# Two-layer graph attention: broadcast rows through DRAM in place of TensorE, with signs and roots moved in the order of the queues

## The chip, the core and the metric

The kernel runs on one core of one Trainium2 chip. The metric is the device time of one execution in microseconds. Three runs of the kernel before gave 2392.19, 2395.01 and 2395.21 us, median 2395.01 us. The span in a profile is the time from its first to its last instruction; times in views of the trace count from the span's start.

## What is computed

There are 16 graphs of 1024 nodes with 256 features, one adjacency matrix for all. Each graph goes through a layer normalization and a first network (a matmul to 512 features, a dense attention over all nodes, a matmul back to 256, an attention masked by the adjacency), is added to its input, and then goes through a second normalization and a second masked attention. Cut to what matters:

```python
def _gat(inp, adj_mask, W, a):
    h = jnp.matmul(inp, W)
    f1 = jnp.matmul(h, a[:F_, 0])
    f2 = jnp.matmul(h, a[F_:, 0])
    e = leaky_relu(f1[:, :, None] + f2[:, None, :], ALPHA)
    if adj_mask is not None:
        e = jnp.where(adj_mask[None] > 0, e, NEG_INF)
    return jnp.einsum('bij,bjf->bif', softmax(e, axis=2), h)   # then elu

# network 0 of a graph
out = relu(x @ mlp1_w + mlp1_b)
out = elu(elu(_gat(out, None, W_fc, a_fc))) + out
out = relu(out @ mlp2_w + mlp2_b)
out = relu(elu(elu(_gat(out, adj, W_hand, a_hand))) + out)
# whole: x = x + net0(relu(layernorm(x))); x = x + net1(relu(layernorm(x)))
```

Here net1 is one masked attention with its own W and a, and relu at the end. All is in float32.

## The kernel before, in words

**Tiles.** A graph's 1024 nodes are eight tiles of 128 partitions (`NT = 8`), in two halves of four (`NH = 2`, `TH = 4`). Each graph passes through these objects: `Norm` (two of them), `Dense` (first matmul, dense attention, second matmul), `Gnn0` (masked attention a) and `Gnn1` (masked attention b).

**The masked attentions** need, for every node i, the factor q of i as a row that is the same on all 128 partitions: `weight` (L356, DVE) makes a tile of weights from that row, two columns and the mask `edge`, and `product` (L367, PE) multiplies it by the rows of h. The row is made by `row` (L343): `row_broadcast` (L236) transposes each of eight columns of 128 values, spread over 128 columns, on PE into PSUM, and ACT copies the result to SBUF (L347). Ahead of it stand `extremes` (the largest and smallest f2 on each partition, L318 and L319) and `vectors`: two transposes spread these over all partitions, two reductions on DVE (L328, L329) take the extremes of all, three small exponentials on ACT make the columns `qwd`. The smallest f2 is used only in `trouble`, a flag that is looked at after the last graph.

**The dense attention** of graphs 1 to 15 (and half of graph 0) has no product over all pairs. Nodes are ranked by f2: `columns` (L456) takes f2 as a column, `row` (L460) spreads it as the row `r2` by the same eight transposes and an ACT copy (L466), and finds the largest; `rank` (L484 to L491, DVE, three passes over r2 for each of eight tiles) counts the smaller ones; `scatter` (L498, POOL, indirect DMA) writes the rows of h in sorted order to DRAM; `read_sorted` (L544, SP) reads them back. DVE makes running sums from both ends (L575, L592); SP writes them to DRAM as a table (`write_table`, L584), with carries between partitions (`carry`, L600 to L604). `sign` (L522, ACT, eight times a graph) counts for every node how many f2 lie above minus its f1, from the same r2; `count` (L528) turns this into an index; `gather` (L615, POOL, indirect DMA) fetches from the fine table and then adds from the coarse one; `share` and `mean` (L627 to L639) make the result, and `merge` (L686) transposes it.

**The order of work** is written by hand. `at(lo, hi, steps)` puts steps on a table with nominal times, in us; the table is sorted and the steps are issued in that order, and the instructions of PE, DVE, ACT and SP stay in it. POOL's are chained by hand in the same order (only scatters may pass each other). So every engine and SP's queue take their instructions strictly in the order of the nominal times, and each waits only for its inputs and for free buffers. `PERIOD` is 142: in the period of graph b, PE works on the masked attention a of graph b, the masked attention b of graph b - 1, and parts of the dense attentions of graphs b + 1 and b + 2. The first period is shorter by 28. The lines that place what the change touches:

```python
def dense_begin(t0, b):
    d = dense[b]
    at(t0 - 38.5, t0 - 38.5, [d.columns])
    at(t0 - 31.5, t0 - 31.5, [d.row])
    at(t0 - 28, t0 - 12, each(d.rank, range(NT)))
```

`dense_begin` serves graphs 2 to 15; graphs 0 and 1 have their own lines at the start. In `second_norm` the last two graphs have their own lines too, so `vectors` and `row` of b are split over two periods for graphs 0 to 13. `masked_first` places the two roots of the second norm (`Norm.root`, L257 and L258, POOL) at 36 and 46.5 of graph 0's period; in that period the coarse gathers of the second half stood from 34 on. DVE's `center` (L262) needs the root, and PE's `turn` (L272) needs `center`.

**Buffers.** The rows r2, the rows of a and the rows of b share one tag, `rows`, with two buffers in turn: a row takes the buffer of the row two before it. Matmul results have four PSUM buffers (`mm`), transposes two (`tr`), broadcasts one (`bc`). Weights have eight (`att`).

Of the kernel before, what the change touches and what calls it, by code (L numbers as in the profile page):

```python
# [17 lines left out]
P = 128  # L18
# [13 lines left out]
def fast_path(ctx: ExitStack, tc: tile.TileContext, alarm, x, adj, w1, b1, w2, b2, w_fc, a_fc,  # L32
# [148 lines left out]
    coarse_d = [dram.tile([P + 1, 2 * K], F32, name=f"coarse{k}") for k in range(2)]  # L181
    zero = work.tile([1, K], F32, tag="carry", name="zero", bufs=2)
    nc.vector.memset(zero, 0.0)
    for k in range(2):
        for s in range(2):
            nc.sync.dma_start(fine_d[k][N:N + 1, s * K:(s + 1) * K], zero)
            nc.sync.dma_start(coarse_d[k][s * P:s * P + 1, s * K:(s + 1) * K], zero)

# [44 lines left out]
    def row_broadcast(dst, col):  # L233

        for u in range(len(col)):
            nc.tensor.transpose(dst[:, u * P:(u + 1) * P], col[u].to_broadcast([P, P]), ident)  # L236

# [54 lines left out]
    class Masked:  # L292
# [3 lines left out]
        def __init__(self, get_hT, w_sb, slope, b, which):  # L296
            self.get_hT, self.w_sb, self.slope, self.name = get_hT, w_sb, slope, f"{which}_{b}"
            self.hm = None
            self.att = {}
            self.out = {}  # L300
# [20 lines left out]
        def vectors(self):  # L321
# [4 lines left out]
            row_broadcast(ext_ps[:, :2 * P], cols(self.ext))  # L326
            top = small.tile([P, 4], F32, tag="top", name=f"top{self.name}")
            nc.vector.tensor_reduce(top[:, 0:1], ext_ps[:, :P], AX.X, OP.max)  # L328
            nc.vector.tensor_reduce(top[:, 1:2], ext_ps[:, P:2 * P], AX.X, OP.min)  # L329
# [4 lines left out]
            nc.vector.scalar_tensor_tensor(trouble[:, 1:2], top[:, 0:1], top[:, 1:2],  # L334
# [8 lines left out]
        def row(self):  # L343
            rows_ps = bc_psum(f"rowsps{self.name}")
            row_broadcast(rows_ps, cols(self.qwd[:, 0, :]))
            self.rows = work.tile([P, N], F32, tag="rows", name=f"rows{self.name}")
            nc.scalar.copy(self.rows, rows_ps)  # L347
# [67 lines left out]
    class Dense:  # L415
# [44 lines left out]
        def row(self):  # L460

            b, ext = self.b, self.ext
            r2_ps = bc_psum(f"r2ps_{b}")
            row_broadcast(r2_ps, cols(self.fs[:, 1, :]))
            self.r2 = work.tile([P, N], F32, tag="rows", name=f"r2_{b}")
            nc.scalar.copy(self.r2, r2_ps)  # L466
# [9 lines left out]
            self.place = small.tile([P, NT], I32, tag="place", name=f"place_{b}")  # L476

# [32 lines left out]
        def query(self):  # L510

            f1 = self.fs[:, 0, :]
            self.q = small.tile([P, NT], F32, tag="qd", name=f"qd_{self.b}")
            nc.vector.tensor_scalar(self.q, f1, self.top[:, 0:1], 0.0, op0=OP.add, op1=OP.max)
            nc.scalar.activation(self.q, self.q, AF.Exp, scale=SLOPE_A - 1.0)
            self.signs = small.tile([P, NT], F32, tag="signs", name=f"signs_{self.b}")
# [259 lines left out]
    def dense_begin(t0, b):  # L776
        d = dense[b]
        at(t0 - 38.5, t0 - 38.5, [d.columns])
        at(t0 - 31.5, t0 - 31.5, [d.row])
# [11 lines left out]
    def dense_sums(t0, b):  # L791
        d = dense[b]
        at(t0 - 3, t0 - 3, [d.sums_begin])
        at(t0 + 8.5, t0 + 28, each(d.sign, range(NT)))
# [64 lines left out]
    def second_norm(t0, b):  # L859
# [62 lines left out]
    at(START + 54.2, START + 54.2, [d.row])  # L922
# [28 lines left out]
    at(START + 98.5, START + 98.5, [e.row])  # L951
# [23 lines left out]
    for b in range(NB):  # L975
# [491 lines left out]
```

## Time and profile before

| what | value |
|---|---|
| median of three runs | 2395.01 us |
| the profiled execution's own time | 2395.08 us |
| its span | 2393.4 us, granted TensorE clock 0.987 |
| r2: PE transposes L236, then ACT copy L466 | 128 of 272 ns busy; 16 of 1012 ns |
| rows of b: PE transposes, then ACT copy L347 | 128 of 273 ns busy; 16 of 995 ns |
| extremes: PE transposes for a and for b | 32 of 275 ns and 32 of 276 ns busy |
| reductions of the smallest, L329 | 16 of 281 ns for a, 16 of 281 ns for b |
| sign L522 | 124 of 1146 ns |
| rank passes L484, L486, L488 | 740, 806 and 352 ns |
| gathers L615, fine and coarse | 124 of 1093 ns and 124 of 1577 ns on POOL |
| PE waits in all, centering before a transpose (L272 for L262) | 27.6 us, 20 times, longest 10.4 us |
| SP's DMA queue, packets and share of 16 engines' span | 97440, 24.5% |

A line of a group gives the line of the code, engine, operation, output and inputs, count, busy time and the mean of one, then the idle time of the engine just before these instructions and what ended it. Matmuls overlap, so the busy time of one (272 ns) is more than the distance from one start to the next. A line of a timeline gives start and length in us, engine, line, operation, and in brackets the idle time before it with its releaser. PEld is the load of weights of PE, which runs beside its matmuls. A stretch's line gives its length, the busy time of each engine with counts, then PE's clock, the DMA engines' busy share and GB/s.

### The profile page before, as it was taken

Reading aid. Unit: us, or ns where it says so; the run is one execution under the profiler, and the core shown is the slowest. Engines: PE = TensorE matmul, PEld = TensorE weight load, DVE = VectorE, ACT = ScalarE, POOL = GpSimd, SP = SyncE. Lnnn points to the kernel's source line nnn. Section 1 sums busy time; section 2 is a strip of 40 time slices with the busy share of each in tenths; the row PEclk is TensorE's granted clock in tenths of the full one; section 3 lists DMA queues with packets and bytes.
Section 4 is the critical chain, followed back from the end, with each engine's and each line's share of the span. In section 5 each row is a group of like instructions: output and inputs, shape, how many; then the busy total and the mean of one; then the engine's idle time right before and its main releaser. Section 6 shows DMA issues by size and latency. Waiting matters only on the chain. (4 is left out here: it accounts for less than half of the span.)

```text
span 2393.4 us, 31270 instructions
## 1 busy us (share of the span) xinstructions
PE 2311.4 (97%) x10281; PEld 1788.2 (75%) x10281; DVE 1635.3 (68%) x4531; ACT 1286.1 (54%) x2740; POOL 977.9 (41%) x1216
## 2 busy tenths in 40 slices
PE   8988899999999999999999999999999999999897
PEld 5666687787777878777777868777787877878676
DVE  6665586676858667685866858577685867759554
ACT  4355565545656554565645556564555655455442
POOL 1153335363443536344353533535443453634220
PEclk9999999999999999999999999999999999999898
DMA  4548257372654827356382645737264573726500
GB/s 170 166 141 212 44 153 191 108 190 78 170 143 138 206 89 189 89 153 169 124 220 89 168 97 151 185 122 196 78 182 110 156 189 108 191 74 193 115 1 28
DMA packets 143562, 333.62 MB, mean 139 GB/s; under 512 B 9624, under 2 KB 60824, under 8 KB 139296
## 3 DMA queue, kind: packets, MB, share of 16 engines
q0 software_dynamic: 45952, 163.99, 25.6%
q1 hardware_dynamic: 97440, 167.56, 24.5%
q8 instruction: 84, 1.38, 0.3%
q14 instruction: 86, 0.70, 0.1%
HBM read 205.38 MB, written 126.12 MB: 139 GB/s over the span
## 5 line engine op out<-in xcount | busy, mean ns | idle before, releaser
L367 PE MATMUL oa<-hma,atta 128*128 128x258 f32 x2048 | 459.7, 383 | 7.0 <-DVE atta L356 4.4
L448 PE MATMUL h<-wfc_sb,resT 128*128 128x257 f32 x2048 | 464.6, 380 | 0.0
L367 PE MATMUL ob<-hmb,attb 128*128 128x257 f32 x2048 | 458.3, 383 | 5.4 <-DVE attb L356 5.4
L367 PEld LDWEIGHTS oa<-hma,atta 128*128 128x128 f32 x2048 | 385.6, 191 | 71.9 <-DVE atta L356 10.5
L367 PEld LDWEIGHTS ob<-hmb,attb 128*128 128x128 f32 x2048 | 391.2, 192 | 61.6 <-ACT hmb L351 3.7
L448 PEld LDWEIGHTS h<-wfc_sb,resT 128*128 128x128 f32 x2048 | 379.8, 190 | 52.3 <-issue 1.0
L697 POOL TENSOR_TENSOR resT<-resT,e 128x512 f32<-128x512 f32 x128 | 163.1, 1274 | 415.9 <-DVE e L696 371.9
L356 DVE SCALAR_TENSOR_TENSOR atta<-rowsa,qwda,edge 128x256 f32<-128x256 f32 x512 | 251.2, 519 | 45.2 <-ACT rowsa L347 30.8
L356 DVE SCALAR_TENSOR_TENSOR attb<-rowsb,qwdb,edge 128x256 f32<-128x256 f32 x512 | 257.3, 531 | 30.9 <-PE ob L367 21.4
L391 POOL TENSOR_TENSOR posa<-posa,onat 128x256 f32<-128x256 f32 x120 | 101.0, 841 | 390.2 <-ACT posa L383 390.2
L434 PE MATMUL m<-hT,w_sb 128*128 128x512 f32 x512 | 238.8, 602 | 0.5 <-ACT posa L383 0.5
L704 PE MATMUL m<-resT,w_sb 128*128 128x512 f32 x512 | 230.5, 597 | 4.4 <-POOL resT L697 4.4
L615 POOL DMA_INDIRECT got<-coarse,k x124 | 195.6, 1577 | 42.5 <-issue 36.2
L405 ACT ACTIVATE rb<-ob,recb 128x256 f32<-128x256 f32 x128 | 57.4, 474 | 268.5 <-DVE recb L403 249.0
L688 DVE TENSOR_SCALAR e<-hpT 128x512 f32<-128x512 f32 x128 | 88.4, 691 | 145.7 <-PE hpT L686 144.5
L704 PEld LDWEIGHTS m<-resT,w_sb 128*128 128x128 f32 x512 | 94.1, 192 | 105.8 <-issue 94.3
L450 ACT COPY hnat<-h 128x257 f32<-128x257 f32 x256 | 92.1, 365 | 143.4 <-PE h L448 128.4
L382 ACT ACTIVATE ea<-oa,reca 128x256 f32<-128x256 f32 x128 | 60.6, 473 | 192.9 <-DVE reca L379 192.9
L615 POOL DMA_INDIRECT got<-fine,k x124 | 135.6, 1093 | 68.4 <-DVE reca L379 33.1
L434 PEld LDWEIGHTS m<-hT,w_sb 128*128 128x128 f32 x512 | 93.1, 194 | 84.6 <-issue 82.3
L498 POOL DMA_INDIRECT sorted<-hnat,place x128 | 131.8, 1030 | 39.3 <-issue 16.3
L392 POOL TENSOR_TENSOR ea<-ea,posa 128x256 f32<-128x256 f32 x120 | 112.1, 934 | 85.0 <-ACT ea L389 67.4
(179 smaller groups left out, 3615.6 us busy)
## 6 DMA issues: line engine op xcount, KB each, us to landing
xs<-sorted SPq DMA_DIRECT2D x32, 1028.0 KB
fine<-tt SPq DMA_DIRECT2D x15, 2052.0 KB
fine<-xs SPq DMA_DIRECT2D x15, 2052.0 KB
x<-in_x_dram SPq DMA_DIRECT2D x16, 1024.0 KB
out_dram<-x SPq DMA_DIRECT2D x32, 512.0 KB
xn<-in_x_dram SPq DMA_DIRECT2D x15, 1024.0 KB
coarse<-carry SPq DMA_DIRECT2D x32, 256.5 KB
fine<-tt SPq DMA_DIRECT2D x2, 1026.0 KB
```

The source lines that it names most:

```text
L356: nc.vector.scalar_tensor_tensor(a_t, self.rows[:, q * PAIR:(q + 1) * PAIR], self.qwd[:, 1, j:j + 1], edge[:, j, q * PAIR:(q + 1) * PAIR], ...
L367: nc.tensor.matmul(self.out[t][:, :F + self.ONES], lhsT=self.att[q, j][:, (t % 2) * P:(t % 2 + 1) * P], rhs=self.hm[:, j, 2:2 + F + self.O ...
L391: adder.tensor_add(pos, pos, o_nat[:, t, :])
L392: adder.tensor_add(e, e, pos)
L434: nc.tensor.matmul(ps, lhsT=w1_sb[:, kc, c * P:(c + 1) * P], rhs=hT[:, kc, h * HALF:(h + 1) * HALF], start=(kc == 0), stop=(kc == FC - 1))
L448: nc.tensor.matmul(ps[:, :F + 1], lhsT=self.resT[:, kc, t * P:(t + 1) * P], rhs=wfc_sb[:, kc, g, :], start=(kc == 0), stop=(kc == HC - 1))
L450: nc.scalar.copy(self.h_nat[:, t, g, :], ps[:, :F + 1])
L498: made = nc.gpsimd.indirect_dma_start(out=sorted_d[self.b % 2], out_offset=bass.IndirectOffsetOnAxis(ap=self.place[:, t:t + 1], axis=0), i ...
L615: nc.gpsimd.indirect_dma_start(out=got[u // n][:, u % n, :], out_offset=None, in_=(coarse_d if coarse else fine_d)[self.b % 2][:, :], in_o ...
L688: nc.vector.tensor_scalar_min(e, ps, 0.0)
L697: nc.gpsimd.tensor_add(dst, dst, e)
L704: nc.tensor.matmul(ps, lhsT=w2_sb[:, kc, c * P:(c + 1) * P], rhs=self.resT[:, kc, h * HALF:(h + 1) * HALF], start=(kc == 0), stop=(kc == H ...
```

## The change

Four things are changed.

- For graphs 2 to 15 the row r2, and for graphs 0 to 13 the row of b, is made through DRAM: `send` has SP write the column of 1024 values to a DRAM row of 4 KB, and `row(True)` has SP read that row to all 128 partitions. Both sends are issued right after the values are made; r2 is read at once (38.5 before the period's end, where the transposes stood at 31.5), the row of b at 22 of the next period, where its transposes stood at 31.5. The largest f2 is split off into `highest`, which keeps the old place. The row of a stays on PE.
- In `vectors` the smallest f2 is no more transposed and reduced: the flag takes each partition's own smallest value.
- `sign` of a graph goes from 8.5 to 28 after the period's start to 22 to 4 before it.
- In graph 0's period the coarse gathers of the second half go from 34 to 47, behind both roots.

Cut to its core:

```diff
@@ fast_path
+    row_d = {s: [dram.tile([1, N], F32, name=f"row_{s}{k}") for k in range(2)] for s in "rb"}
+    def send_row(dst, col):
+        nc.sync.dma_start(dst.rearrange("o (u i) -> i (o u)", i=P), col)
@@ Masked.vectors
-            row_broadcast(ext_ps[:, :2 * P], cols(self.ext))
+            row_broadcast(ext_ps[:, :P], [self.ext[:, 0:1]])
-            nc.vector.tensor_reduce(top[:, 1:2], ext_ps[:, P:2 * P], AX.X, OP.min)
-            nc.vector.scalar_tensor_tensor(trouble[:, 1:2], top[:, 0:1], top[:, 1:2],
+            nc.vector.scalar_tensor_tensor(trouble[:, 1:2], top[:, 0:1], self.ext[:, 1:2],
@@ Masked
-        def row(self):
-            rows_ps = bc_psum(f"rowsps{self.name}")
-            row_broadcast(rows_ps, cols(self.qwd[:, 0, :]))
+        def send(self):
+            send_row(row_d["b"][self.b % 2], self.qwd[:, 0, :])
+        def row(self, sent=False):
             self.rows = work.tile([P, N], F32, tag="rows", name=f"rows{self.name}")
-            nc.scalar.copy(self.rows, rows_ps)
+            if sent:
+                nc.sync.dma_start(self.rows, row_d["b"][self.b % 2].to_broadcast([P, N]))
+            else:
+                rows_ps = bc_psum(f"rowsps{self.name}")
+                row_broadcast(rows_ps, cols(self.qwd[:, 0, :]))
+                nc.scalar.copy(self.rows, rows_ps)
@@ Dense
+        def send(self):
+            send_row(row_d["r"][self.b % 2], self.fs[:, 1, :])
-        def row(self):
+        def row(self, sent=False):
+            self.r2 = work.tile([P, N], F32, tag="rows", name=f"r2_{self.b}")
+            if sent:
+                nc.sync.dma_start(self.r2, row_d["r"][self.b % 2].to_broadcast([P, N]))
+            else:
+                r2_ps = bc_psum(f"r2ps_{self.b}")
+                row_broadcast(r2_ps, cols(self.fs[:, 1, :]))
+                nc.scalar.copy(self.r2, r2_ps)
+        def highest(self):
             b, ext = self.b, self.ext
             ...
@@ dense_begin
-        at(t0 - 38.5, t0 - 38.5, [d.columns])
-        at(t0 - 31.5, t0 - 31.5, [d.row])
+        at(t0 - 38.5, t0 - 38.5, [d.columns, d.send, partial(d.row, True)])
+        at(t0 - 31.5, t0 - 31.5, [d.highest])
@@ dense_sums
-        at(t0 + 8.5, t0 + 28, each(d.sign, range(NT)))
+        at(t0 - 22, t0 - 4, each(d.sign, range(NT)))
@@ second_norm, graphs 0 to 13
-            at(lo + 11, lo + 11, [m.vectors])
+            at(lo + 11, lo + 11, [m.vectors, m.send])
-            at(base_of(b + 1) + 31.5, base_of(b + 1) + 31.5, [m.row])
+            at(base_of(b + 1) + 22, base_of(b + 1) + 22, [partial(m.row, True)])
@@ the loop over graphs, gathers
-                lo = base + (16 if b == 0 else 48 + 4 * h)
-                gathers(dense[b + 1], h, lo + 12 * h, lo + 6 + 12 * h) if b == 0 else gathers(
-                    dense[b + 1], h, lo, base + 58 + 7 * h)
+                if b:
+                    gathers(dense[b + 1], h, base + 48 + 4 * h, base + 58 + 7 * h)
+                else:
+                    gathers(dense[1], h, base + 16 + 12 * h, base + 22 + 25 * h)
```

For graphs 0 and 1 the calls become `[d.row, d.highest]` at the old places. The tile of `signs` is made in `highest` in place of `query`.

More of the change, by code (lines that the diff above doesn't have):

```diff
@@ L297, in __init__ @@
             self.get_hT, self.w_sb, self.slope, self.name = get_hT, w_sb, slope, f"{which}_{b}"
+            self.b = b
             self.hm = None
@@ L458, in columns @@
             nc.vector.tensor_reduce(self.ext, self.fs[:, 1, :], AX.X, OP.max)
-        def row(self):
+        def send(self):
[9 more added lines that the diff above has]
+        def highest(self):
             b, ext = self.b, self.ext
[L463 to L466, printed above, removed]
             ext_ps = tr_psum(f"extdps_{b}")
@@ L476, in row @@
             self.place = small.tile([P, NT], I32, tag="place", name=f"place_{b}")
+            self.signs = small.tile([P, NT], F32, tag="signs", name=f"signs_{b}")
         def rank(self, t):
@@ L515, in query @@
             nc.scalar.activation(self.q, self.q, AF.Exp, scale=SLOPE_A - 1.0)
-            self.signs = small.tile([P, NT], F32, tag="signs", name=f"signs_{self.b}")
         def sign(self, t):
@@ L921, in fast_path @@
     at(START + 51.5, START + 51.5, [d.columns])
-    at(START + 54.2, START + 54.2, [d.row])
+    at(START + 54.2, START + 54.2, [d.row, d.highest])
     at(START + 54.5, START + 71, each(d.rank, range(NT)))
@@ L950, in fast_path @@
     at(START + 95.5, START + 95.5, [e.columns])
-    at(START + 98.5, START + 98.5, [e.row])
+    at(START + 98.5, START + 98.5, [e.row, e.highest])
     at(START + 99, START + 118, each(e.rank, range(NT)))
```

## The prediction

> **What bounds the kernel now.** I read the page's busy shares first, then stretches of one period, then the idle gaps of TensorE (PE), then, in the steady period from 565 us, each engine's timeline.
>
> ```profile
> PE 2311.4 (97%) x10281; PEld 1788.2 (75%) x10281; DVE 1635.3 (68%) x4531; ACT 1286.1 (54%) x2740; POOL 977.9 (41%) x1216
> ```
>
> ```profile
> 233.00:262.00 29.00, 16.67 (x70) 12.64 (x70) 10.34 (x35) 10.81 (x25) 9.52 (x10) 0.76 0.66 162
> ...
> 472.00:614.00 142.00, 141.09 (x634) 109.64 (x633) 99.28 (x276) 80.10 (x171) 62.65 (x77) 1.00 0.52 145
> ```
>
> The second view gives, for a stretch, its length and the busy time of PE, PEld, DVE, ACT and POOL, then PE's clock. In the 142 us stretch PE is idle for 0.9 us: the repeated period is bound by PE, and PE work taken out should shorten it until another engine is next. The stretch from 233 us is different: 12.3 us idle, and the clock down to 0.76. The three timelines show why (PE, then DVE, then POOL):
>
> ```profile
> 243.73 1.76 PE L272 MATMUL nt<-ident,hn 128*128 128x128 f32 x6 [10.42 <-DVE hn L262]
> ```
>
> ```profile
> 243.26 0.74 DVE L262 TENSOR_SCALAR hn<-x,mv,rstd 128x256 f32<-128x256 f32 x2 [9.89 <-POOL rstd L258]
> ```
>
> ```profile
> 238.39 1.56 POOL L615 DMA_INDIRECT got<-coarse,k  x1 [5.05 <-DMA got<-fine,k]
> 240.25 1.54 POOL L615 DMA_INDIRECT got<-coarse,k  x1 [0.30 <-issue]
> 241.26 0.83 POOL L257 TENSOR_SCALAR rstd<-mv 128x4 f32<-128x4 f32 x1
> ```
>
> POOL takes its queue in order: the root that DVE needs stands behind two coarse gathers, the first of which waits 5.05 us for the fine gathers to land. Now the steady period, on DVE, ACT and PE:
>
> ```profile
> 623.31 0.93 DVE L396 SCALAR_TENSOR_TENSOR x<-ea,x 128x256 f32<-128x256 f32 x1 [0.62 <-POOL ea L392]
> ...
> 633.80 0.47 DVE L356 SCALAR_TENSOR_TENSOR atta<-rowsa,qwda,edge 128x256 f32<-128x256 f32 x1
> ```
>
> ```profile
> 627.81 1.15 ACT L522 ACTIVATE junk<-r,fs 128x1024 int8<-128x1024 f32 x1
> ```
>
> ```profile
> 569.23 1.03 PE L236 MATMUL r2ps<-ident,fs 128*128 128x128 f32 x8
> ...
> 627.94 1.04 PE L236 MATMUL rowspsb<-ident,qwdb 128*128 128x128 f32 x8
> 628.81 0.60 PE L367 MATMUL oa<-hma,atta 128*128 128x258 f32 x2
> 629.83 4.18 PE L367 MATMUL oa<-hma,atta 128*128 128x258 f32 x18 [0.42 <-ACT posa L383]
> 634.32 2.88 PE L367 MATMUL oa<-hma,atta 128*128 128x258 f32 x12 [0.31 <-DVE atta L356]
> ```
>
> A broadcast of eight transposes holds PE for 628.81 - 627.94 = 0.87 us, 0.11 us a transpose. At 634.32 PE already waits for DVE's weights, so there DVE is the next limit.
>
> **What the skill says.** "DMA: Bandwidth & Descriptors", Anatomy of one DMA: about 2.0 us are fixed per transfer, whatever its size, plus bytes over 436 GB/s (fitted on the GpSimd path). The trace agrees roughly: the read of sorted rows starts at 602.18 on SP and its first half of 1028 KB lets ACT go at 607.20, 5.0 us, where the formula gives 4.4. Same page, Specifications: below 512 B a transfer costs a read-modify-write; no run here stores 4-byte pieces, so this is open. "TensorE: Matmul & The Clock Gate", What's actually happening: PE's clock halves after an idle window of about 3.4 us and needs as much busy time to return. The trace agrees: the granted clock over 237.11 to 250.77 is 0.50. "SBUF — State Buffer", SBUF: two separate sides: DVE operations with two SBUF inputs and GpSimd exclude each other; the trace has L396 at 0.93 us beside POOL and 0.41 us away from it.
>
> **The change, part by part.**
>
> *Row r2 through DRAM (graphs 2 to 15, 14 times).* Off PE: 8 transposes, 0.87 us, and ACT's copy L466, 1.01 us. PE is without a gap there, so 14 x 0.87 = 12.2 us come off if the row is in time. What is added: SP sends 1024 words as 4-byte pieces, waits for them to land, and reads 512 KB to all partitions. SP is empty then (in the period shown from the load at 529.89 us to the read of sorted rows at 602.18), so nothing is queued behind that wait. Room: in the period before that one, the column is made on DVE at 422.11 to 422.27, and the first rank starts at 431.75; it would start 0.87 us sooner, at 430.88. That leaves 8.6 us. Behind that rank on DVE stand a second rank and the four centerings, for which PE already waits 0.20 us (nt at 577.44): each us of lateness costs PE a whole us per period. Cost of the send: 64 pieces on each of 16 DMA engines. In 6.4 to 7.9 us, when the biases are loaded as 4-byte pieces, 816 packets under 512 B pass, 51 an engine in 1.5 us among bigger ones, so 29 ns a piece at most: 1.9 us, with the fixed 2.0 us an estimate of 3.9. Low end: the pieces hide in the fixed part, 2.0. High end: every piece costs as much as the mean packet of SP's queue (24.5% of 16 x 2393 us over 97440 packets, 96 ns): 6.2 + 2.0 = 8.2. The read: 2.0 + 524288/436e3 = 3.2 by the page, and with the 0.6 us by which the trace was above it 3.8. Chain: 7.7 (5.2 to 12.0). I take 7.7: in time by 0.9 us.
>
> *Row of gnn1 through DRAM (14 times).* Off PE 0.87 us, off ACT L347, 1.0 us. The send follows the vectors some 80 us before use and has no deadline. The read stands on SP behind the table write of 2052 KB (issued 615.54; its traffic ends at about 626) and before the next one at 633. With 3.8 us it lands near 630, at worst; DVE asks for the row at 635.73. The buffer is that of r2, free because the signs are done. Hidden; were it not, DVE's weights and PE's products of gnn1 would wait.
>
> *Signs (L522) moved ahead.* Eight of 1.15 us leave ACT between 609 and 629 and enter between about 577 and 593, where ACT's copies of h come every 1.73 us and take 0.37: 1.3 us fit in between. The last sign waits for POOL's copy of f1, at 590.75, perhaps 0.5 us; ACT's hma copies queue behind it and PE has four PSUM buffers, so zero for PE (0.5 us a period if the cover is gone). What it frees: posa for PE's gap at 629.83 comes 1.15 us sooner (the 0.42 goes), and ea for DVE's gap at 623.31 (the 0.62 goes).
>
> *The two together at 606 to 637.* PE's side gets 0.87 + 0.42 us shorter, DVE's only 0.62 us. PE waits at 634.32 for the weight that DVE makes at 633.80, so what is won there is 0.62 us plus little: I take 0.66, with 0.4 to 1.6 as ends (DVE slower or faster beside POOL).
>
> *f2's minimum without a transpose.* 32 transposes of 0.11 us, 32 reductions of 0.28 us. In the 14 periods one of the two counts, 0.11; at the end of the run, where PE waits out the chain extremes, vectors, row (three times), 0.11 + 0.2 us each, 0.9 together, and 0.4 elsewhere.
>
> Per period: 0.87 + 0.11 + 0.66 = 1.64; times 14 = 23.0 us. One-offs of this kind: 1.3 us.
>
> *Roots ahead of gathers (once).* POOL's last fine gather ends at 233.34, the inputs of the root are there since 228.6, so root 0 ends near 234.7 (0.24 + 1.04 us), and PE's transposes start at 235.3 in place of 243.73: 8.4 us. The gap of 2 us that stays may halve the clock for one window instead of 13.66 us with 6.41 us of PE work; I count 1 to 2 us more. What is late next: root 1 must wait for statistics (2.9 us later on DVE) and blocks the coarse gathers until 239.1; four at 1.85 us end at 246.5, where they ended at 247.04, while their reader (share, 264.99) comes only to 255. So 9.5 us, 7 to 12.
>
> Sum: 23.0 + 1.3 + 9.5 = 33.8 us. The profiled execution took 2395.08 us (span 2393.4), the median of the runs shown is 2395.01, so no correction: 2395.0 - 33.8 = 2361.
>
> **Rivals.** Within 0.2% is about what a measurement of this kernel can tell from no change: 2390.2 to 2399.8.
> - A, as above: 2361, own range 2352 to 2370. Chance 0.62.
> - B, DVE takes more: nothing is won at 606 to 637 beyond 0.1 us and the gap gives 6. 14 x 1.08 + 1.3 + 6 = 22.4: 2373. For it speaks the DVE stream without a gap from 607 to 635; against it that ACT's signs delay that stream by 0.62. Chance 0.12.
> - C, PE gets all: 14 x (0.87 + 0.11 + 0.87 + 0.73) + 1.3 + 11 = 48: 2347. For it: DVE waits 3.25 us for the sorted rows ahead of that stream, so it might move up. Chance 0.12.
> - D, the row r2 is late, one mechanism with one place: the first rank, period after period. It decides from 8.6 us on; at 11.0 us (2.4 late, 14 x 2.4 = 34) all is lost, at the high end of 12.0 us it costs 47.6: 2361 + 47.6 = 2409, slower. For it: stores of 4 bytes are shown nowhere here, and the skill warns of them; against it: idle DMA engines (share 0.00 from 418 to 426 us). Chance 0.07 for slower, 0.04 for within 0.2%, 0.03 for faster by less than B.
> - The change does not do what it says: the built program's order has PE without both broadcasts from graph 2 on and both sends at the empty place of SP; I give this nothing.
>
> **Numbers.** Faster 0.62 + 0.12 + 0.12 + 0.03 = 0.89, within 0.04, slower 0.07. The range leaves out D and the far edge of C: 2347 to 2378.
>
> **What would show it.** Right: no r2ps after graph 1 and no rowsb copy from PSUM; the first rank of a period without a wait for a DMA; nt with 0.2 us; the gap at 233 us shrunk to about 2 us; periods of about 139.7 us in place of 141.3; the wait of oa for posa gone and that for atta grown. Wrong: DVE waiting at L486 for the row by DMA and PE at nt by as much (D); hma late on ACT with PE waiting at pa; attb waiting for its row; share of period one waiting for coarse gathers.

## The result, and the profile after

The changed kernel takes 2472.91 us (median of four runs, 2466.32 to 2483.14) against 2393.6 us for the kernel before on the same chip: ratio 1.0338, 95% interval 1.0294 to 1.0382. It is slower by 79 us; the forecast was 2361, and rival D had this side. The profiled execution took 2466.32 us, its span is 2464.5 us.

The page's busy times, then two stretches of the changed kernel (length, busy time of PE, PEld, DVE, ACT, POOL, then PE's clock, DMA share, GB/s):

```profile
PE 2305.0 (94%) x10025; PEld 1779.3 (72%) x10025; DVE 1635.6 (66%) x4499; ACT 1252.3 (51%) x2712; POOL 967.2 (39%) x1216
```

```profile
230.00:262.00 32.00, 25.81 (x117) 20.06 (x116) 17.64 (x46) 18.19 (x38) 15.95 (x15) 0.89 0.75 169
472.00:614.00 142.00, 133.76 (x580) 104.16 (x579) 95.99 (x265) 70.85 (x155) 62.50 (x77) 0.98 0.52 134
```

PE has 256 instructions less and still only 6.4 us less busy time, because some of it now runs at a lower clock (the granted clock is 0.50 over the 4 us from 587.5, see below). The first stretch, that of period one, got better, as forecast: PE is idle for 6 us and not for 12. The second, a whole period, got worse: 8.2 us idle in place of 0.9. So the loss recurs in each period. The chain that ended last (part 4 of the page) names it:

```profile
PE 57%; DVE 20%; DMA 13%; ACT 4%; POOL 3%; issue 2%; DVEq 0%; POOLq 0%; ACTq 0%; SPq 0%
PE h L461 16%; PE oa L380 9%; PE ob L380 7%; PE m L447 7%; DMA row_r<-fs 6%; PE pa L318 4%; DVE attb L369 4%; DVE atta L369 4%; PE pb L318 3%; DMA got<-coarse,k 3%; POOL got L637 3%; PE m L726 3%; DMA r<-row_r 3%; PE nt L278 3%; DVE xs L614 2%
```

The send and the read of r2 are 9% of the chain. In one period (from 566 us), on SP's queue, then DVE, then PE; last, PE in the same place of the kernel before:

```profile
568.17 0.36 SPq L242 DMA_DIRECT2D row_r<-fs  x1
579.57 0.33 SPq L480 DMA_DIRECT2D r<-row_r  x1
```

```profile
583.28 1.28 DVE L509 TENSOR_SCALAR_CACHE_REDUCE junk<-r,fs 128x1024 uint8<-128x1024 f32 x1 [6.45 <-DMA r<-row_r]
```

```profile
587.75 1.94 PE L278 MATMUL nt<-ident,hn 128*128 128x128 f32 x8 [6.76 <-DVE hn L268]
589.48 12.32 PE L461 MATMUL h<-wfc_sb,resT 128*128 128x257 f32 x48
```

```profile
577.44 1.32 PE L272 MATMUL nt<-ident,hn 128*128 128x128 f32 x8 [0.20 <-DVE hn L262]
578.59 10.56 PE L448 MATMUL h<-wfc_sb,resT 128*128 128x257 f32 x48
```

SP issues the send at 568.17 and the read, which waits for it, at 579.57: the send took 11.4 us to be known as landed. In the 14 periods it took 8.66 to 11.40 us, and the first rank started 13.9 to 15.1 us after the send. Where the send was known sooner (8.7 to 9.7 us, seven periods) the read took longer, 5.3 to 5.4 us from its issue to the first rank; behind sends of 10.1 to 11.4 us it took 3.6 to 4.2. DVE stands for 6.45 us at that rank, and PE for 6.76 us at the transposes behind it. Then the same matmuls of h take 12.32 us; before, with a wait of 0.20 us ahead of them, they took 10.56. From nt's start to pa's start it is 11.56 us in every period of the kernel before, and 12.71 to 14.09 (mean 13.16) in the changed one. Over these 13 periods nt waits 6.07 us on average, before 0.20. Per period 5.87 + 1.60 = 7.5 us, times 13 = 97 us lost. The fourteenth row is late too (DVE waits 7.78 us for it), but no nt stands behind its ranks; there PE waits 2.16 us at pa, for ACT's hma, which stands behind a value that DVE makes after the ranks. What that period loses in all isn't told apart from other differences at the end of the run.

The DMA view of 566 to 582 us says what the engines did in those 11.4 us (40 slices of 0.4 us: busy tenths, then GB/s):

```profile
DMA  0000000272000000000000000000000000007799
GB/s 0 0 0 0 0 0 0 2 7 2 0 0 0 0 0 0 0 0 0 0 0 0 0 0 0 0 0 0 0 0 0 0 0 0 0 0 113 236 369 389
DMA packets 1148, 0.45 MB, mean 28 GB/s; under 512 B 1040, under 2 KB 1040, under 8 KB 1148
```

The send's packets pass in slices 8 to 10, 0.9 to 1.6 us after its issue. Then nothing moves for some 10 us. The time is not in the packets, but between the last of them and the landing. Of all waits (in all, times, longest), these answer to the forecast's list, first of the changed kernel, then of the kernel before:

```profile
PE nt L278 <- DVE hn L268: 98.0, 20, 9.9
PE oa L380 <- DVE atta L369: 11.4, 27, 0.6
```

```profile
PE nt L272 <- DVE hn L262: 27.6, 20, 10.4
PE oa L367 <- DVE atta L356: 4.4, 14, 0.3
PE oa L367 <- ACT posa L383: 2.6, 13, 0.4
```

The wait of oa for posa is gone and that for atta has grown, as forecast; nt has grown, as rival D said.

### The profile page after: what moved, and what is told of

The parts are those of the page before. It is cut to its first block, busy times and chain, and to the rows that moved or that the text cites. A ratio compares the mean times of both kernels' runs of the same rounds, so it can differ in the third digit from the quotient of the medians.

```text
span 2464.5 us, 30883 instructions
## 1 busy us (share of the span) xinstructions
PE 2305.0 (94%) x10025; PEld 1779.3 (72%) x10025; DVE 1635.6 (66%) x4499; ACT 1252.3 (51%) x2712; POOL 967.2 (39%) x1216
## 4 chain that ended last, share of the span: by engine, by line
PE 57%; DVE 20%; DMA 13%; ACT 4%; POOL 3%; issue 2%; DVEq 0%; POOLq 0%; ACTq 0%; SPq 0%
PE h L461 16%; PE oa L380 9%; PE ob L380 7%; PE m L447 7%; DMA row_r<-fs 6%; PE pa L318 4%; DVE attb L369 4%; DVE atta L369 4%; PE pb L318 3%; DMA got<-coarse,k 3%; POOL got L637 3%; PE m L726 3%; DMA r<-row_r 3%; PE nt L278 3%; DVE xs L614 2%
## 5 line engine op out<-in xcount | busy, mean ns | idle before, releaser
L461 PE MATMUL h<-wfc_sb,resT 128*128 128x257 f32 x2048 | 477.8, 388 | 0.0
L380 PE MATMUL oa<-hma,atta 128*128 128x258 f32 x2048 | 457.4, 383 | 11.4 <-DVE atta L369 11.4
L461 PEld LDWEIGHTS h<-wfc_sb,resT 128*128 128x128 f32 x2048 | 391.0, 195 | 56.1 <-issue 1.0
L369 DVE SCALAR_TENSOR_TENSOR atta<-rowsa,qwda,edge 128x256 f32<-128x256 f32 x512 | 263.3, 542 | 47.3 <-ACT rowsa L360 33.0
L404 POOL TENSOR_TENSOR posa<-posa,onat 128x256 f32<-128x256 f32 x120 | 106.7, 889 | 437.8 <-ACT posa L396 437.8
L278 PE MATMUL nt<-ident,hn 128*128 128x128 f32 x512 | 86.9, 318 | 101.1 <-DVE hn L268 98.0
L710 DVE TENSOR_SCALAR e<-hpT 128x512 f32<-128x512 f32 x128 | 88.3, 690 | 139.9 <-PE hpT L708 135.3
L637 POOL DMA_INDIRECT got<-fine,k x124 | 129.7, 1046 | 78.8 <-DVE ea L405 35.6
L278 PEld LDWEIGHTS nt<-ident,hn 128*128 128x128 f32 x512 | 69.4, 162 | 124.5 <-issue 89.8
L509 DVE TENSOR_SCALAR_CACHE_REDUCE junk<-r,fs 128x1024 uint8<-128x1024 f32 (+7 forms) x128 | 103.5, 809 | 83.4 <-DMA r<-row_r 82.6
```

What stands on the lines that cost most here:

```text
L278: nc.tensor.transpose(self.ps[c][:, u * P:(u + 1) * P], self.hn[t][:, c * P:(c + 1) * P], ident)
L369: nc.vector.scalar_tensor_tensor(a_t, self.rows[:, q * PAIR:(q + 1) * PAIR], self.qwd[:, 1, j:j + 1], edge[:, j, q * PAIR:(q + 1) * PAIR], ...
L380: nc.tensor.matmul(self.out[t][:, :F + self.ONES], lhsT=self.att[q, j][:, (t % 2) * P:(t % 2 + 1) * P], rhs=self.hm[:, j, 2:2 + F + self.O ...
L404: adder.tensor_add(pos, pos, o_nat[:, t, :])
L461: nc.tensor.matmul(ps[:, :F + 1], lhsT=self.resT[:, kc, t * P:(t + 1) * P], rhs=wfc_sb[:, kc, g, :], start=(kc == 0), stop=(kc == HC - 1))
L509: nc.vector.tensor_scalar(junk[:, t * P:], r2[:, t * P:], s, None, op0=OP.is_lt, op1=OP.add, accum_out=rank[:, 1, t:t + 1])
```

## The experiments

The experiments ran on four chips. Every ratio is to runs of the kernel before on the same chip, whose median was 2390.3 to 2398.8 us. Line numbers are those of the kernel run.

### r2 back on TensorE

```diff
-        at(t0 - 38.5, t0 - 38.5, [d.columns, d.send, partial(d.row, True)])
-        at(t0 - 31.5, t0 - 31.5, [d.highest])
+        at(t0 - 38.5, t0 - 38.5, [d.columns])
+        at(t0 - 31.5, t0 - 31.5, [d.row, d.highest])
```

> The changed kernel with only the row r2 of graphs 2 to 15 back on TensorE (columns at 38.5, transposes and largest at 31.5 before the period's end); the row of b through DRAM, the signs ahead, f2's minimum and the roots stay as changed. Theory (the send of r2 lands late, everything else in the change pays): the waits of nt for hn return to about 0.2 us a period, the half clock after them goes. In the changed kernel each of 14 periods lost about 6.6 us of waiting and 2.4 us of half clock, 126 us in all, and still the whole was only 79 us over the kernel before, so the rest of the change is worth about 47 us, of which 12 are r2's transposes: expected 2393.6 - 47 + 12 = 2359 us (2350 to 2372). Rival (the signs between ACT's copies of h, or the read of the row of b, cost time too): 2385 us or more, with PE waiting at pa or ob.

Measured: 2384.03 us, ratio 0.9946 (0.9929 to 0.9963). With r2 on PE the rest of the change is faster than the kernel before, and pa's waits do not grow: the loss is r2's path. The gain, 14.7 us (9 to 17), is less than I expected. My 126 us came from the one period shown; the 13 periods together lost 97. And against the forecast some 7 us are missing: 33.8 less the 12.2 of r2's transposes is 21.6. "Where the rest went" takes this up.

### r2 through DRAM alone

The kernel before with `send`, `row(True)` and `highest` for r2 and nothing else:

```diff
-        at(t0 - 38.5, t0 - 38.5, [d.columns])
-        at(t0 - 31.5, t0 - 31.5, [d.row])
+        at(t0 - 38.5, t0 - 38.5, [d.columns, d.send, partial(d.row, True)])
+        at(t0 - 31.5, t0 - 31.5, [d.highest])
```

> The kernel before with one part of the change alone: the row r2 of graphs 2 to 15 through DRAM. Theory: the same late first rank as in the changed kernel, 6 to 7 us of waiting at nt and a half clock after it in each period, without the other parts' gain of about 35 us: 2473 + 35 = 2508 us (2490 to 2520). Rival (the loss needs the parts together, for instance signs and ranks meeting): about 2380 to 2400 us, with little waiting at the first rank.

Measured: 2501.48 us, 1.0431 (1.0405 to 1.0457): 103 us are lost by this part alone. The loss doesn't need the other parts.

### The same row, sent in pieces of 512 B

```diff
-        at(t0 - 38.5, t0 - 38.5, [d.columns, d.send, partial(d.row, True)])
+        at(t0 - 41, t0 - 41, [d.columns])
+        at(t0 - 39.3, t0 - 39.3, [d.send, partial(d.row, True)])
@@ Dense.send
-            send_row(row_d["r"][self.b % 2], self.fs[:, 1, :])
+            ps = bc_psum(f"turn_{b}")
+            nc.tensor.transpose(ps[:NT, :P], self.fs[:, 1, :], ident)
+            line = work.tile([NT, P], F32, tag="carry", name=f"line_{b}", bufs=2)
+            nc.vector.tensor_copy(line, ps[:NT, :P])
+            nc.sync.dma_start(row_d["r"][b % 2].rearrange("o (u i) -> (o u) i", i=P), line)
```

> The changed kernel with another send of r2: the column of 128 x 8 is turned by one transpose on TensorE into 8 partitions of 128, copied to SBUF by DVE, and SP writes it as 8 pieces of 512 B in place of 1024 of 4 B; the column is made a little earlier (41 before the period's end) and sent about 1.6 us sooner than in the changed kernel. The read is the same. Theory (the landing of 4-byte pieces is what is slow): the read is issued 2 to 3.5 us after the send in place of 8.7 to 11.4, the first rank has its row before it asks, no wait at nt beyond about 0.2 us: 2473 - 126 + 2 = 2348 us (2340 to 2362). Rival (the read that spreads 4 KB to 512 KB is the slow part, or the DRAM round trip as such): the rank still starts some 14 us after the send and the time stays above 2400 us.

Measured: 2374.72 us, 0.9904 (0.9877 to 0.993). The same bytes to the same row, and the same read. On SP, DVE and PE:

```profile
553.87 0.29 SPq L479 DMA_DIRECT2D row_r<-line  x1
555.14 0.33 SPq L485 DMA_DIRECT2D r<-row_r  x1
```

```profile
564.04 1.25 DVE L514 TENSOR_SCALAR_CACHE_REDUCE junk<-r,fs 128x1024 uint8<-128x1024 f32 x1
```

```profile
568.48 1.31 PE L278 MATMUL nt<-ident,hn 128*128 128x128 f32 x8 [0.20 <-DVE hn L268]
569.63 10.57 PE L461 MATMUL h<-wfc_sb,resT 128*128 128x257 f32 x48
```

The send lands in 1.27 us (1.2 to 1.3 in all), the rank has no wait in its brackets, nt is back at 0.20 and h at 10.57. The difference to the changed kernel is 1.0338 - 0.9904 = 0.0434 of 2394, 104 us: the whole loss. The read is not the slow part. The column is made earlier here too, but that isn't what mends it: 4-byte pieces sent just as early are still late (next run), and pieces of 32 B sent at the change's own place are in time (further below). The Trainium skill fits this: "DMA: Bandwidth & Descriptors", Latency and other measured facts, puts the least round trip to HBM at about 0.8 us and says that the receipt from memory makes most of a transfer's fixed cost; the second probe below has 1.07 to 1.17 us for a single 512 B store.

### Earlier, with 4-byte pieces

```diff
-        at(t0 - 38.5, t0 - 38.5, [d.columns, d.send, partial(d.row, True)])
+        at(t0 - 41, t0 - 41, [d.columns, d.send, partial(d.row, True)])
```

> The changed kernel with its 4-byte send kept and only moved: column, send and read of r2 at 41 before the period's end in place of 38.5, where DVE is free some 3.8 us sooner. Theory (the row is simply late, and what is late costs TensorE one for one): the wait at nt falls from 6.6 to about 2.8 us a period, the half clock after it goes with it; against the turned send (2375 us) 14 times 2.6 us remain, less the waits behind the gathers that it hides: 2386 to 2412 us, 2400 taken. Rival (the chain is blocked until some other traffic is over, not by its own length): the first rank starts as late as before, 2465 to 2475 us.

Measured: 2407.87 us, 1.005 (1.0031 to 1.007). The landing is as slow as before, the wait is shorter:

```profile
554.10 0.36 SPq L242 DMA_DIRECT2D row_r<-fs  x1
565.41 0.33 SPq L480 DMA_DIRECT2D r<-row_r  x1
```

```profile
573.23 1.67 PE L278 MATMUL nt<-ident,hn 128*128 128x128 f32 x8 [2.45 <-DVE hn L268]
574.69 11.75 PE L461 MATMUL h<-wfc_sb,resT 128*128 128x257 f32 x48
```

It is lateness, paid one for one: the send is 3.9 us sooner, and nt waits 1.8 to 2.8 us (2.25 on average) in place of 6.07. Two thirds of the clock's loss stay (1.06 of 1.60 us a period), which I had not expected: from nt to pa it takes 11.56 us in 4 of 13 periods and 12.69 to 13.25 in the other 9, gaps of 1.87 and of 2.05 us among these. The idle window of about 3.4 us that the forecast took from the Trainium skill ("TensorE: Matmul & The Clock Gate", What's actually happening) is no safe bound here; the measurement decides.

### Probes of sends and reads

Two kernels, each the kernel before with this added in each of graphs 2 to 15, seven forms of store in turn (and, not shown, a few stores at the start that fill the DRAM tiles):

```diff
+            nc.sync.dma_start(<a form of near, apart or wide>, <f2 or a tile>)
+            seen = work.tile([P, N], F32, tag="rows", name=f"seen_{self.b}")
+            nc.sync.dma_start(seen, src.to_broadcast([P, N]))
+            nc.sync.dma_start(note, seen[0:1, :P])
+            nc.sync.dma_start(seen[0:1, :P], note)
```

> The kernel before with a chain of four transfers added on SP in the quiet place of each of graphs 2 to 15 (r2 itself stays on TensorE, nothing waits for the chain): a store to DRAM of one of seven kinds, then a read of 4 KB spread to 128 partitions (512 KB), then a store of 512 B from one partition, then a read of 512 B. Each waits for the one before it to land, so that the distances between their issues on SP are the landings. Kinds, in turn over the graphs: 0 the send of the change (1024 pieces of 4 B into 4 KB, neighbours from neighbouring partitions); 1 the same pieces 64 B apart; 2 the same pieces 512 B apart; 3 128 pieces of 32 B; 4 8 pieces of 512 B; 5 128 pieces of 512 B; 6 128 pieces of 4 B into 512 B. Theory (many small pieces, [...]worst where they share a line): kind 0 takes 8.7 to 11.4 us, kind 4 and the single 512 B about 2 to 2.5, kinds 3 and 5 2.5 to 3.5, kind 6 2.5 to 4; kinds 1 and 2 tell whether sharing of lines counts (then 3 to 5) or the number of pieces (then 8.7 to 11.4 as kind 0). The read takes 3.5 to 4 us after every kind. Rival (the read is the slow part): all sends land in about 2 to 4 us by themselves and the read takes 8 or more.

> A second chain of sends as in the first probe, other kinds, each now made from values that the period has just computed: 0 8 pieces of 512 B; 1 128 pieces of 512 B; 2 128 pieces of 4 B, 64 B apart; 3 the same 16 B apart; 4 the same 8 B apart; 5 1024 pieces of 4 B, 16 B apart; 6 32 pieces of 4 B side by side. Before: 128 pieces of 4 B side by side took 7.3 to 7.8 us, 1024 side by side 11.0 to 12.0, 1024 pieces 64 B apart 2.9 to 4.1, 128 pieces of 32 B 1.4 to 1.5. Theory (what costs is that several pieces from different DMA engines fall into the same 64 B, not their number): kinds 0, 1 and 2 take 1.2 to 2 us, kind 3 3 to 5, kind 4 4 to 7, kind 5 5 to 9, kind 6 3 to 8. Rival (the shared unit is 512 B or more): kind 2 as slow as side by side, 6 us or more. Rival (number of pieces in the same 4 KB): kinds 2, 3 and 4 alike, kind 5 as kind 0 of the first probe.

Both left the time of the kernel as it was (2401.11 and 2396.16 us, one run each). In the first probe kinds 4 and 5 depended on nothing from the period and went out beside the table writes; the second has them again. SP's queue for kind 0 and for kind 3 of the first probe:

```profile
282.29 0.37 SPq L472 DMA_DIRECT2D near<-fs  x1
294.24 0.33 SPq L494 DMA_DIRECT2D seen<-near  x1
298.06 0.25 SPq L495 DMA_DIRECT2D note<-seen  x1
...
706.44 0.34 SPq L481 DMA_DIRECT2D near<-fs  x1
707.86 0.33 SPq L494 DMA_DIRECT2D seen<-near  x1
```

The first three lines give 11.95 us for the send and 3.82 for the read, the last two 1.42 us for the send. All, as the time from the store's issue to the read's:

| store | us (two graphs) |
|---|---|
| 1024 pieces of 4 B side by side, as in the change | 11.95, 11.04 |
| 128 of 4 B side by side | 7.81, 7.33 |
| 32 of 4 B side by side | 3.36, 3.44 |
| 1024 of 4 B, 16 B apart | 3.88, 3.36 |
| 1024 of 4 B, 64 B apart; 512 B apart | 2.85, 4.08; 2.77, 2.55 |
| 128 of 4 B, 8 B apart | 3.15, 2.85 |
| 128 of 4 B, 16 B apart; 64 B apart | 1.43, 3.34; 1.47, 1.42 |
| 128 of 32 B | 1.42, 1.48 |
| 8 of 512 B; 128 of 512 B | 1.22, 1.23; 1.55, 1.60 |

The number of pieces is the lesser part: 1024 of them 512 B apart land in under 2.8 us, 128 side by side need over 7.3. What is slow is many 4-byte pieces that touch each other. The rival "number of pieces" falls, and so does "512 B is the shared unit": 128 pieces 64 B apart, eight to each 512 B, land in 1.42 to 1.47 us, like 128 pieces of 32 B. That the shared unit is exactly 64 B, or which part of the memory path orders them, the runs don't tell. The read takes 3.3 to 4.1 us after most kinds, 4.5 to 4.7 after some stores of pieces 8 or 16 B apart, and 5.2 to 5.5 after 128 or 32 side by side.

### Pieces of 32 B, without a transpose

```diff
-            send_row(row_d["r"][self.b % 2], self.fs[:, 1, :])
+            nc.sync.dma_start(row_d["r"][self.b % 2].rearrange("o (i u) -> i (o u)", i=P), self.fs[:, 1, :])
@@ Dense.row, then rank
+                self.by_tile = self.r2.rearrange("p (i u) -> p u i", u=NT)
-            r2, rank = self.r2, self.ranks
+            r2, rank = self.by_tile, self.ranks
```

> The changed kernel with the send of r2 in the order of the partitions: each partition's eight values go as one piece of 32 B, 128 pieces, into the same 4 KB, with no transpose; the row then holds node tile and partition in the other order, and the ranks read it with a stride of 32 B (the signs only sum over it). Send and read stand where the change has them. Theory (only pieces of 4 B side by side are slow): the read is issued 1.4 to 1.6 us after the send, the first rank has its row in time; if DVE reads with the stride as fast as without, the time is that of the turned send less its transposes, 2373 us (2366 to 2380). Rival (DVE is slower on the strided row: ranks of 0.74 and 0.81 us become longer): the ranks delay the centerings, PE waits at nt, 2385 us or more.

Measured: 2465.48 us, 1.0317 (1.0293 to 1.0341): the rival. The send lands in 1.40 to 1.46 us in 12 of 14 periods (3.2 and 3.6 in the others), and the first rank, 8.6 us after the send, has no wait for its row: the send stands where the change has it, so it is the form of the store that made the row late. But the ranks are slow. DVE's first pass of a graph here:

```profile
570.46 2.03 DVE L512 TENSOR_SCALAR_CACHE_REDUCE junk<-r,fs 128x1024 uint8<-128x1024 f32 x1
```

With the turned send it is the one of 1.25 us shown above: the stride makes it 1.6 times as long. PE pays at nt (1.95 us in each of 13 periods) and more at pa, where ACT's hma, behind the ranks again, costs 40.8 us in 15 waits. The Trainium skill fits the slow pass ("SBUF — State Buffer", Door 1: The DMA port swizzle): lines of 16 B, so that a stride of more than four float32 costs; here it is eight, and the trace agrees. A cheap store can make the reader dear.

### One part at a time

Roots ahead of gathers, in the kernel before:

```diff
-                gathers(dense[b + 1], h, lo + 12 * h, lo + 6 + 12 * h) if b == 0 else gathers(
-                    dense[b + 1], h, lo, base + 58 + 7 * h)
+                if b:
+                    gathers(dense[b + 1], h, base + 48 + 4 * h, base + 58 + 7 * h)
+                else:
+                    gathers(dense[1], h, base + 16 + 12 * h, base + 22 + 25 * h)
```

> The kernel before with the reordering of POOL in period one alone (coarse gathers of the second half behind both roots). The forecast said 9.5 us (7 to 12). In the profiles of the other runs with this part TensorE's gap there is 4.5 to 5.4 us in place of 10.4 and the first transposes of hpT come 6.9 to 9.0 us sooner, the signs' 0.7 to 2.3 us among it: I expect 6.5 us (5 to 9), 2387 us. Rival (given back later, since the coarse gathers of this half end later and their reader waits): 2391 or more.

Measured: 2387.57 us, 0.9969 (0.9957 to 0.998), 8.0 us (4.8 to 10.3).

The row of gnn1 through DRAM alone:

```diff
-            at(lo + 11, lo + 11, [m.vectors])
+            at(lo + 11, lo + 11, [m.vectors, m.send])
-            at(base_of(b + 1) + 31.5, base_of(b + 1) + 31.5, [m.row])
+            at(base_of(b + 1) + 22, base_of(b + 1) + 22, [partial(m.row, True)])
```

> The kernel before with the row of gnn1 (graphs 0 to 13) through DRAM alone; signs, roots, r2 and f2's minimum as before. Its 4-byte send has some 80 us. Theory (the forecast's: PE's part of the window 606 to 637 gets 0.87 us shorter, but DVE is the next limit, and with the signs still on ACT there its weights come no sooner): at most 0.3 us a period, 2390 to 2395 us, the wait of oa for atta grown by 0.5 us or more a period. Rival (PE gets all of it): 14 times 0.87, 2382 us.

Measured: 2393.06 us, 1.0008 (0.9999 to 1.0016). PE lost eight transposes a period and gained nothing; what it waits for is ACT, busy with signs:

```profile
625.91 4.18 PE L381 MATMUL oa<-hma,atta 128*128 128x258 f32 x18 [1.05 <-ACT posa L397]
```

The 0.42 us of before became 1.05, and over the run this wait grew from 2.6 to 14.2 us, about what the transposes had freed. The forecast's theory held in the time; the wait that grew is that for posa, not for atta.

Signs ahead alone:

```diff
-        at(t0 + 8.5, t0 + 28, each(d.sign, range(NT)))
+        at(t0 - 22, t0 - 4, each(d.sign, range(NT)))
```

> The kernel before with the signs ahead alone (eight of 1.15 us a graph leave ACT between 8.5 and 28 after the period's start and go between 22 and 4 before it). Theory (the forecast's): the wait of oa for posa (0.42 us a period) goes and DVE's stream in the window gets 0.62 us shorter: 0.5 us a period, 2394 - 7 = 2387 us (2384 to 2391). Rival (the signs cost as much where they go, hma late at PE): 2393 us or more, with waits at pa.

Measured: 2383.4 us, 0.9967 (0.9954 to 0.9979), 8 us. The wait for posa is gone, and the shortest periods are 140.72 us; before they are 141.22.

### Where the rest went

In the kernel with r2 on TensorE the shortest periods are 140.5 us, with the turned send 139.7, as the forecast's steps give; but every second one or so is 0.3 to 2.0 us longer. The longer ones have a wait that the others have not (r2 on TensorE, PE, then POOL of the same period):

```profile
814.96 0.29 PE L238 MATMUL extpsb<-ident,extb 128*128 128x128 f32 x1 [1.69 <-DVE extb L326]
```

```profile
781.66 1.09 POOL L637 DMA_INDIRECT got<-fine,k  x1 [2.11 <-DMA fine<-xs]
```

PE waits for extremes that stand on DVE behind a share, the share behind the coarse gathers, and these behind the fine gathers, which start 2.11 us late because the second table write has not landed. I first took the gathers' order for the cause, with the turned send:

```diff
-                    gathers(dense[b + 1], h, base + 48 + 4 * h, base + 58 + 7 * h)
+                    d, t = dense[b + 1], base + 48 + 4 * h
+                    at(t, t + 4 - 2 * h, each(d.gather, [h], [0], range(TH - 2 * h)))
+                    at(base + 64.9, base + 64.9, each(d.gather, [1], [0], range(TH - 2 * h, TH)))
+                    at(base + 58 + 7 * h, base + 65 + 7 * h, each(d.gather, [h], [1], range(TH)))
```

> The turned-send kernel with POOL's gathers in another order in graphs 2 to 15: the last two fine gathers of the second half go behind the coarse gathers of the first half, so that the first half's results land some 2.6 us sooner. Theory (what the forecast lost beside the send went into a new wait: TensorE comes sooner to extpsb and hpT, whose inputs stand on DVE behind the landing of the coarse gathers; in the kernel with r2 on TensorE and with the turned send these waits cost 5 to 7 us over the run, and they turn up only in some periods): the waits of extpsb for extb go, periods come near the shortest ones of the turned-send kernel (139.7 us, mean 140.5), 2375 - 6 = 2369 us (2364 to 2372). Rival (the coarse gathers of the first half then wait for the landing of the fine ones, POOL stands, the second half is late at its merge): no gain or slower, 2374 to 2385 us.

Measured: 2374.83 us, 0.9909 (0.9893 to 0.9926), no gain over the turned send: the steady waits of extpsb went, those of hpT for hp grew from 7.4 to 10.4 us, and POOL stood 65.9 us in all, up to 6.1 at a time, until fine gathers had landed. Then the write itself, with the turned send:

```diff
-            at(base_of(b + 1) + 22, base_of(b + 1) + 22, [partial(m.row, True)])
+            at(base_of(b + 1) - 10, base_of(b + 1) - 10, [partial(m.row, True)])
```

> The turned-send kernel with one thing more: the read of gnn1's row (512 KB) goes from 22 after the start of the period to 10 before it, the quiet place of SP's queue, out of the stretch between the two table writes of 2052 KB. Theory (in the kernels that have signs and row both as changed, the row's read stands right behind the first table write[...], so that the second table write, and with it the first fine gather on POOL, comes up to 2 us later than POOL asks; the coarse gathers, the shares and TensorE's extpsb and hpT follow): POOL's waits for the table write go, the waits of extpsb too, the periods come near 139.7 us each in place of 140.45 on average: 14 times 0.7, so 8 to 10 us less than the turned send, about 0.987 of the kernel before, 2364 us (2359 to 2369). Rival (the gathers are late for another reason, for instance TensorE simply comes sooner): no change, 0.990 of the kernel before, 2371 to 2375 us. Rival (the early read delays r2's own, just ahead of it): waits at nt, 2380 us or more.

Measured: 2362.29 us against 2390.31, 0.9878 (0.9861 to 0.9894), the best kernel of this study. POOL has no wait for the table write, and 10 of 12 periods take 139.7 to 139.9 us. But that the moved read did this is not shown. The interval overlaps that of the turned send, and this run was on another chip, on which no kernel had the read at its old place. Runs that share a chip speak against the theory. These are POOL's waits for the table write from 300 us on, for the turned send, then for r2 through DRAM alone and for the first probe; all three ran on one chip (a in the table below), and the last two have no read of gnn1's row:

```profile
POOL got L642 <- DMA fine<-xs: 17.4, 12, 2.5
POOL got L638 <- DMA fine<-xs: 7.9, 5, 2.2
POOL got L653 <- DMA fine<-xs: 8.9, 7, 1.5
```

On chip c, the pieces of 32 B, with the read 0.7 us behind the first table write as in the turned send, then the signs alone, without it:

```profile
POOL got L640 <- DMA fine<-xs: 0.8, 1, 0.8
POOL got L638 <- DMA fine<-xs: 1.1, 1, 1.1
```

Most of the difference on chip a is the signs': with them ahead, POOL asks 14.27 us after the second write's issue in place of 14.80, so a late landing shows sooner. Counted from 14.27 us in every kernel, the first fine gathers of 14 graphs start late by so much in all (in brackets the longest time from the write's issue to the gather; us):

| chip (its kernel before) | read right behind the first write | no read there |
|---|---|---|
| a (2398.75) | r2 on TensorE 14.5 (16.4), turned send 16.2 (16.6) | r2 alone 12.7 (16.8), first probe 15.6 (16.2) |
| b (2395.59) | earlier send 11.5 (16.3), other order of gathers 8.6 (15.7) | roots alone 6.7 (16.0), second probe 9.5 (16.2) |
| c (2391.55) | pieces of 32 B 1.3 (14.9) | signs alone 1.0 (15.2), row alone 0 (14.8) |
| d (2390.31) | none run | early read 0.1 (14.3) |

In the kernels that ask at 14.80, up to 0.53 us a graph is unseen, so their sums are low ends. The write lands late on two chips and hardly on the others, with the row's read or without it. So what decides differs from chip to chip (the chip itself, or where a run's tables lie in its DRAM; the runs don't tell), and the 6 us between 0.9904 and 0.9878 can't be given to the moved read. That the write is late mostly in every second period, while two tables take turns, points to the place in DRAM, but that is only argued. The turned send and the early read on one chip would tell; that wasn't run.

## Why the prediction was wrong, step by step

- **The send of r2.** This step failed: 3.9 us (2.0 to 8.2) was forecast, 8.7 to 11.4 measured, past the high end. I built it from the time of packets (29 ns a piece, from loads). The packets cost even less, 0.7 us for all 1024. But SP waits for the landing, which for these 4-byte stores that touch comes 7 to 10 us after the last packet. No number of a load's packets could bound that; the range should not have ended at a packet's mean.
- **The read**, 3.8 us: measured 3.3 to 4.1 in most probes, right. In the changed kernel it took 3.6 to 5.4, more where the send was known sooner, so the slow store is felt in the read as well.
- **Lateness costs PE one for one.** Right (3.9 us sooner, 3.8 us less waiting), and so were the mechanism and place of rival D, which was given a chance of 0.07 for slower: chain 13.9 to 15.1 us against room of 8.6. Its size was off twice: the chain, and the clock after the gap (1.6 us a period), which it left out. Hence 2473 and not 2409.
- **Eight transposes of r2, 0.87 us a period.** Right: from 140.5 to 139.7 us, with the turned send's own transpose of 0.11 in it.
- **Row of gnn1: hidden.** Nothing speaks against it: no weight attb waits for the row. Alone the part gives nothing, because PE then waits for ACT. The forecast didn't ask what the read does to the write behind it; by the table above, nothing that can be told from the differences between chips.
- **Signs free for PE; window 0.66 us.** About right: 0.5 us a period from the signs alone, none from the row, and no new wait for hma.
- **f2, 0.11 us a period.** The shortest periods with row and f2 added to the signs are 0.12 to 0.2 us shorter. Consistent; too small to show alone.
- **Roots, 9.5 us (7 to 12).** Measured 8.0 (4.8 to 10.3), in range. In the changed kernel's profile POOL and PE:

```profile
232.64 0.94 POOL L637 DMA_INDIRECT got<-fine,k  x1 [0.30 <-issue]
233.61 0.26 POOL L263 TENSOR_SCALAR rstd<-mv 128x4 f32<-128x4 f32 x1
233.96 1.05 POOL L264 TENSOR_TENSOR rstd<-rstd,power 128x4 f32<-128x4 f32 x1
```

```profile
235.52 1.67 PE L278 MATMUL nt<-ident,hn 128*128 128x128 f32 x6 [4.47 <-DVE hn L268]
```

The transposes start at 235.52, forecast 235.3. The gap is 4.47 us and not 2, since PE comes there sooner, and PE's clock is still 0.50 over the 4 us from 235.5, so most of the clock's 1 to 2 us did not come back.

- **The sum.** With the send turned the gain is 23 us (17 to 29), with the row's read early as well 28 us (25 to 33), of 33.8 forecast: apart from the send the steps held in the main. What the missing 6 to 11 us are is open; a part may go with the late table write, which isn't in the forecast at all.

## What to carry to other kernels

Before a small transfer is put on a path with a deadline, ask how its pieces lie where they land, not how many bytes or packets it has: send whole runs (a transpose of 0.11 us and a copy made 1024 pieces into 8 and took the send from 11 to 1.2 us, with 2.4 us from the column to the send), and if no trace shows such a store, measure it with a chain of dependent transfers beside the kernel first. A part that gives nothing alone may hide behind another engine's work, so undo and add parts one by one. And compare them on one chip before a few us are put down to a cause: here the lateness of one and the same table write differed more from chip to chip than from kernel to kernel.

## What the runs showed that was not expected

- 1024 stores of 4 B into 4 KB of DRAM: packets over in 0.7 us, landing known after 8.7 to 12.0 us; 128 of 32 B into the same 4 KB: 1.4 us.
- A PE gap of 1.87 to 2.82 us already cost 1.1 to 1.7 us at a lower clock in 9 of 13 periods (granted 0.58 from 573 to 577 us, around the gap of 2.45 us), and in the others nothing. The length of the gap doesn't decide: with pieces of 32 B it was 1.94 to 1.96 us in all 13 periods, and 7 of them lost 1.4 to 1.7 us.
- A float32 read of 1024 elements on DVE at a stride of 32 B took 2.03 us in place of 1.25.
- The landing of the same 2052 KB write held POOL's gathers up by 7 to 16 us over 14 graphs on two chips and by 0 to 1.3 us on two others, whether a 512 KB read stood right behind the write before it or not.
